# A graph attention layer with gathered rows: E and Q one batch further ahead in two PSUM banks each, the other banks merged

## The chip, the core and the metric

The kernel runs on one NeuronCore of one Trainium2 chip. The metric is the device time of one execution in microseconds, the median of the runs; lower is better. Engines are named as in the profile: PE is TensorE (PEld its weight loads), DVE is VectorE, ACT is ScalarE, POOL is GpSimd, SP is SyncE. PSUM, where PE writes and DVE and ACT read, is used here in eight banks of 128 partitions by 512 float32.

## What is computed

A graph with 6250 nodes of 128 features and 206250 directed edges, sorted by their target node `dst`. Cut to what matters:

```python
Qh = (h @ WQ).reshape(N, 8, 16)          # N = 6250, h = x
Kh = (h @ WK).reshape(N, 8, 16)
Vh = (h @ WV).reshape(N, 8, 16)
Eh = (edge_attr @ WE).reshape(-1, 8, 16) # one row for each edge
score = einsum('ehd,ehd,ehd->eh', Kh[src], Qh[dst], Eh) / sqrt(16)
score = exp(clip(score, -5, 5))
wV = segment_sum(Vh[src] * score[:, :, None], dst)
Z  = segment_sum(score, dst)
x  = layernorm(x + (wV / (Z[:, :, None] + 1e-6)).reshape(N, 128))
```

## The kernel before

**Tiles and batches.** Edges are cut into 1612 tiles of 128, four tiles to a batch (512 edges), 406 batches in all (the last ones are smaller). A table of K and V rows is built in device memory at the start (line 226), and the rows of each edge's source node are fetched from it by `gather` (line 307): four indirect DMAs to a batch, one for each tile, issued by POOL. The first 12 batches (`XB`) fetch rows of x instead and compute K and V themselves in `project` (line 323).

**The loop.** Lines 464 to 516 run over iterations b, and one iteration works on several batches at different stages. Its order on the engines is the order of the calls, written out by hand from b = 12 on (line 466):

- `gather(b)` on POOL (line 475).
- `turn(b-1)` on PE (line 368): four transposes of the product `eq` into a PSUM tile `pps`.
- `stage_a(b)` on PE and ACT (line 348): Q's rows expanded to edges, one matmul into `qps` (line 354), which ACT copies to `qT` in SBUF (line 356); then E, two instructions into `eps` (line 358).
- `finish(q)` in about one of eight iterations (line 404): PE sums the windows of 128 finished nodes into `finps`, ACT copies it to `fin`, and a layernorm of small DVE instructions starts from there (its first writes `rz`, line 604). The layernorm's instructions are dealt out one by one by `fill()`, between the others on DVE, from the next iteration on.
- `stage_b(b-2)` on DVE (line 376): `kq`, the product of gathered K rows and `pps` (line 379), its sum over heads `sc` (382) and the clip (385).
- `messages(b-3)` on DVE (line 411): `msg`, V rows times weights.
- `stage_0(b+AHEAD)` on DVE (line 337): two one-hot matrices, `onehot` (340) for the scatter, `onehotT` (344) for Q.
- `pairs(b)` on DVE (line 361): `eq`, the product of `qT` and `eps` (line 365).
- `weigh(b-2)` on ACT (line 388): two exponentials.
- `stage_c(b-3)` on PE (line 418): the scatter, matmuls of `onehot` and `msg` into `agg` (line 431). A finished sum is copied by ACT (441).
- `q_rows` in about one of eight iterations, always the last thing in its iteration (line 255): Q of 128 more nodes on PE (258), split into three bf16 parts by two ACT casts (261, 263) and two DVE subtractions (262, 264) in turn, and a store to device memory issued by SP (265).

Each engine works through its own instructions in this order; engines wait for each other through semaphores. SP issues all loads ahead of use: `ea` (edge features, six buffers of eight tiles), `relb` (two buffers of sixteen tiles), `qw` (five).

**PSUM banks (lines 207 to 212).** `psE` one bank (`eps`), `psQ` one (`qps`), `psP` two (`pps`), `psT` one, shared under the tag `oT` by `finps`, `qrows`, `project`'s `xtps` and one small count; `psA` two for `agg`, `psX` one for constants.

**The tie (line 317).** From b = 16 on (`LOCK`) the first gather of batch b waits for `expanded[b - lag(b)]`, the Q matmul of line 354 of an earlier batch. `lag` (line 303) falls from 12 at b = 16 by one every four batches down to `STEP` = 1, which it reaches at b = 60. The gathers rotate over `GB` = 17 buffers.

Of the kernel before, what the change touches and what calls it, by code (L numbers as in the profile page):

```python
# [8 lines left out]
F32 = mybir.dt.float32  # L9
# [6 lines left out]
P = 128  # L16
N, E, D, H, DH = 6250, 206250, 128, 8, 16
# [7 lines left out]
MW = D + H  # L25
B = 4
CH = 8
GB = 17
XB = 12
LOCK = XB + 4  # L30
STEP = 1
TAIL = 8
HEAD = 132
NG = (NT + G - 1) // G
AHEAD = 2
EB = 6
SLAG = 2
WT = 8
# [42 lines left out]
def edge_attention(ctx: ExitStack, tc: tile.TileContext, x, xT, srcT, dstT, dstB, dst0, bnd, lo, eaT,  # L81
# [30 lines left out]
    with ExitStack() as fast:  # L112
# [78 lines left out]
        def count_inside():  # L191

            W = 4 * 2 * D
            for a in range(0, NT, W):
                e = min(NT, a + W)
                cl = wp.tile([P, W], F32, name="cl", tag="kvst", bufs=2)[:, :e - a]
                count(P, cl, rel[:, a:e], P - 1)
            nc.vector.tensor_reduce(cn[:, :1], cn, axis=AX.X, op=ALU.add)
            pc = psT.tile([1, 1], F32, name="pc", tag="oT")
            nc.tensor.matmul(pc, cn[:, :1], ones, start=True, stop=True)  # L200
            nc.vector.tensor_copy(cnt_i, pc)

        gp = fast.enter_context(tc.tile_pool(name="gather", bufs=GB))
        ep = fast.enter_context(tc.tile_pool(name="edges", bufs=EB))
        wp = fast.enter_context(tc.tile_pool(name="work", bufs=3))
        sp = fast.enter_context(tc.tile_pool(name="sums", bufs=7))
        psE = fast.enter_context(tc.tile_pool(name="psE", bufs=1, space=bass.MemoryType.PSUM))
        psQ = fast.enter_context(tc.tile_pool(name="psQ", bufs=1, space=bass.MemoryType.PSUM))
        psP = fast.enter_context(tc.tile_pool(name="psP", bufs=2, space=bass.MemoryType.PSUM))
        psT = fast.enter_context(tc.tile_pool(name="psT", bufs=1, space=bass.MemoryType.PSUM))  # L210
        psA = fast.enter_context(tc.tile_pool(name="psA", bufs=2, space=bass.MemoryType.PSUM))
        psX = fast.enter_context(tc.tile_pool(name="psX", bufs=1, space=bass.MemoryType.PSUM))

# [3 lines left out]

        def pair_bank(i, name, shape):

            pool, tag = ((psE, "eps"), (psP, "pps"), (psQ, "qps"), (psP, "pps"))[i % 4]  # L220
            return pool.tile(shape, F32, name=name, tag=tag)


# [24 lines left out]
        nbat = len(batches)  # L248
# [5 lines left out]

        def q_rows(q):
            n = min(P, N - q * P)
            ps = psT.tile([P, D], F32, name="qrows", tag="oT")
            nc.tensor.matmul(ps[:n], xT_sb[:, LEFT + q * P:LEFT + q * P + n], wq_sb, start=True, stop=True)
            st = wp.tile([P, QP, D], BF16, name="qst", bufs=1)
            r1 = wp.tile([P, D], F32, name="qr1", bufs=1)  # L260
            nc.scalar.copy(st[:n, 0, :], ps[:n])  # L261
            nc.vector.tensor_tensor(r1[:n], ps[:n], st[:n, 0, :], op=ALU.subtract)  # L262
            nc.scalar.copy(st[:n, 1, :], r1[:n])
            nc.vector.tensor_tensor(st[:n, 2, :], r1[:n], st[:n, 1, :], op=ALU.subtract)
            nc.sync.dma_start(qs[q * P * QP:(q * P + n) * QP].rearrange("(p s) f -> p s f", s=QP), st[:n])
            built.append(q)
# [20 lines left out]
        chunks, aggs, sums, st8, expanded = {}, {}, {}, {}, {}  # L287
# [15 lines left out]
        def lag(b):  # L303

            return max(STEP, 12 - (b - LOCK) // 4)

# [15 lines left out]

        def project(g, n):

            pt = psT.tile([P, B, P], F32, name="xtps", tag="oT")
            for i in range(n):
                nc.tensor.transpose(pt[:, i, :], g[:, i, :D], ident)
            xgT = wp.tile([P, B, P], F32, name="xgT", tag="kq", bufs=2)
            nc.scalar.copy(xgT[:, :n], pt[:, :n])
            for i in range(0, n, 2):  # L330
                k = min(2, n - i)
                pk = pair_bank(i // 2, "kvps", [P, 2, 2 * D])
                for j in range(k):
                    nc.tensor.matmul(pk[:, j, :], xgT[:, i + j, :], wkv_sb, start=True, stop=True)
                nc.scalar.copy(g[:, i:i + k, :], pk[:, :k, :])

        def stage_0(b):
            t0, n = batches[b][0], len(batches[b])
            oh = wp.tile([P, B, P], F32, name="onehot", bufs=AHEAD + 5)
            nc.vector.tensor_tensor(oh[:, :n], iota_p[:, None, :].to_broadcast([P, n, P]),  # L340
                                    rel[:, t0:t0 + n, None].to_broadcast([P, n, P]), op=ALU.is_equal)
            ohT = wp.tile([QROWS, B * P], BF16, name="onehotT", bufs=AHEAD + 2)
            e0 = t0 % RC * P
            nc.vector.tensor_scalar(ohT[:, :n * P], rels[t0 // RC][:, e0:e0 + n * P], node[:QROWS], None,  # L344
                                    op0=ALU.is_equal)
            st8[b] = oh, ohT

        def stage_a(b, g):
            t0, n = batches[b][0], len(batches[b])
            if b < XB:  # L350
                project(g, n)
            oh, ohT = st8.pop(b)
            pq = psQ.tile([P, B * P], F32, name="qps")
            expanded[b] = nc.tensor.matmul(pq[:, :n * P], loaded[t0 // WT], ohT[:, :n * P], start=True, stop=True)  # L354
            qT = wp.tile([P, B * P], F32, name="qT", bufs=2)
            nc.scalar.copy(qT[:, :n * P], pq[:, :n * P])  # L356
            pe = psE.tile([P, B * P], F32, name="eps")
            nc.tensor.matmul(pe[:, :n * P], we_sb, ea_tiles(t0, n), start=True, stop=True)  # L358
            st8[b] = [n, g, oh, pe, qT]
# [42 lines left out]
                                 start=i == 0, stop=stop and i == len(parts) - 1)  # L402

        def finish(q):
            ps = psT.tile([P, MW], F32, name="finps", tag="oT")
            add_windows(ps, q, True)
            fin = sp.tile([P, MW], F32, name="fin", bufs=2)
            nc.scalar.copy(fin, ps)
            pending.append(layernorm(nc, sp, fin, xbs.pop(q), out, q, stores))
# [36 lines left out]
        gathered = {b: gather(b) for b in range(min(XB, len(batches)))}  # L446
# [11 lines left out]
        def fill():  # L458

            if norms and next(norms[0], None) is None:  # L460
                norms.pop(0)

        held = []
        for b in range(nbat + 4):
            if b >= XB and not manual:
                manual.append(fast.enter_context(tc.manual_schedule()))
            held += [(b + SLAG, store) for store in stores]
            stores.clear()
            if held and (held[0][0] <= b or b >= nbat):
                held.pop(0)[1]()  # L470
            if b < nbat:
                load_chunk(batches[b][0] // CH + EB - 3)
                load_rel(batches[b][0] // RC + 1)
                load_q(batches[b][0] // WT + QLOOK)
                g = gathered.pop(b) if b in gathered else gather(b)
                if b == min(XB, nbat - 1):
                    late_loads()
                if b == min(XB + 8, nbat - 1):
                    relative(C0, NT)
                if b == 14:  # L480
                    from_window(1)
                if b == 0:
                    for i in range(AHEAD):
                        stage_0(i)
                if b > 0:
                    turn(b - 1)
                stage_a(b, g)
            elif b == nbat:
                turn(b - 1)
            norms.extend(pending)  # L490
            pending.clear()
            for q in ready:
                finish(q)
            ready.clear()
            if 0 <= b - 2 < nbat:
                stage_b(b - 2)
            if 0 <= b - 3 < nbat:
                messages(b - 3)
            fill()
            if b + AHEAD < nbat:  # L500
                stage_0(b + AHEAD)
            if b < nbat:
                pairs(b)
            if 0 <= b - 2 < nbat:
                weigh(b - 2)
            if 0 <= b - 3 < nbat:
                stage_c(b - 3)
            fill()
            if b < nbat:
                while len(built) < q_built(min(NJ - 1, batches[b][0] // WT + QLOOK + 2)):  # L510
                    q_rows(len(built))
            if b == min(60, nbat):
                count_inside()
            if b == min(80, nbat + 1):
                inside = nc.values_load(cnt_i[0:1, 0:1], min_val=0, max_val=2 * EPAD,
                                        skip_runtime_bounds_check_because="two counts of EPAD edges")
# [151 lines left out]
```

## Time and profile before

| | |
|---|---|
| runs | 2429.15, 2424.27, 2415.33 us; median 2424.27 us |
| the profiled execution | 2430.0 us, span 2428.1 us, mean granted TensorE clock 0.811 |
| first Q matmul of the loop | 91.3 us after the span's start |
| one batch from b = 60 on, from one `qT` copy to the next | 5.84 us on average |
| one batch from b = 20 to 60 | 5.1 us |
| idle time of DVE before `eq` / `qr` / `rz` | 476.2 / 116.8 / 110.7 us in the whole span |
| mean duration of one `kq`, `sc`, `msg`, `onehot`, `eq` on DVE | 0.68 us each |
| `onehotT` / clip on DVE | 0.36 / 0.20 us |
| one batch on PE at full clock: 4 `pps`, 1 `qps`, 2 `eps`, 8 `agg` | issued over 0.43, 0.22, 0.86 and 0.93 us |

The page's first part is each engine's busy time as a share of the span. No engine is near 100%, so the order of the waits matters, not the sums. Section 5 of the page has the costliest groups of instructions with the idle time before them and what ended it. "remote" there is an event that the profile can't put to an instruction. Matmul ends are modelled by the profiler and not observed.

### The profile page before, as it was taken

What the parts mean: (1) busy time and instruction counts of PE and PEld (TensorE: products, weight loads), DVE (VectorE), ACT (ScalarE), POOL (GpSimd) and SP (SyncE); (2) the same over time, 40 slices, a digit from 0 to 9 for tenths busy, and PEclk for the clock granted to TensorE, in tenths of its full rate; (3) what the DMA queues carried; (4) which work ended last, traced back from release to release, by engine and by line L of the source; (5) the groups of instructions that cost most, each with busy time, mean ns of one, the idle gap of its engine ahead of it and who ended that gap; (6) DMA issues with size and microseconds to landing.
All of it is one profiled execution on the core that took longest, in us unless ns stands there. A gap on an engine that the chain in (4) does not pass through costs nothing.

```text
span 2428.1 us, 24930 instructions
## 1 busy us (share of the span) xinstructions
PE 1539.8 (63%) x6880; PEld 1086.0 (45%) x6880; DVE 1577.4 (65%) x3779; ACT 458.9 (19%) x1572; POOL 1534.0 (63%) x1619
## 2 busy tenths in 40 slices
PE   3587666666665666657666666666666656656665
PEld 2365444444444444444444444444444444444444
DVE  1368778666766666667667666666666667666766
ACT  0232122111111111111111111111111111111111
POOL 7346565666666666666666666666666666666664
PEclk6898898887878888778877878788778788887887
DMA  5645555556554555556456554655555556554642
GB/s 176 201 144 174 179 156 178 165 150 185 170 166 148 168 177 156 164 152 196 147 157 196 160 156 149 184 168 151 169 162 178 147 155 196 157 156 146 197 150 71
DMA packets 178482, 398.16 MB, mean 164 GB/s; under 512 B 61756, under 2 KB 87526, under 8 KB 178336
## 3 DMA queue, kind: packets, MB, share of 16 engines
q0 software_dynamic: 76592, 208.18, 29.4%
q1 hardware_dynamic: 100604, 187.38, 25.2%
q8 instruction: 57, 0.93, 0.2%
q10 hardware_dynamic: 1140, 0.93, 0.1%
q14 instruction: 89, 0.73, 0.1%
HBM read 381.54 MB, written 14.81 MB: 163 GB/s over the span
## 4 chain that ended last, share of the span: by engine, by line
PE 34%; another core or an unknown queue 23%; DVE 19%; issue 16%; ACT 4%; DMA 2%; POOL 1%; DVEq 1%; SPq 0%; ACTq 0%; POOLq 0%
PE agg L431 10%; PE eps L358 10%; PE pps L373 7%; DVE sc L382 4%; DVE kq L379 4%; DVE eq L365 3%; PE qps L354 3%; ACT qT L356 2%; DVE msg L413 2%; PE finps L401 2%; POOL kvrows L314 1%; DVE onehot L340 1%; DVE onehotT L344 1%; DMA kvrows<-kv,src 1%
## 5 line engine op out<-in xcount | busy, mean ns | idle before, releaser
L314 POOL DMA_INDIRECT kvrows<-kv,src x1564 | 1487.1, 951 | 862.3 <-issue 385.6
L431 PEld LDWEIGHTS agg<-msg,onehot 128*128 128x128 f32 x3224 | 516.7, 230 | 664.3 <-issue 520.9
L431 PE MATMUL agg<-msg,onehot 128*128 128x136 f32 x3224 | 560.5, 326 | 352.8 <-DVE msg L413 137.2
L373 PE MATMUL pps<-shift,eq 128*128 128x128 f32 x1612 | 320.5, 332 | 419.6 <-DVE eq L365 238.5
L365 DVE TENSOR_TENSOR eq<-qT,eps 128x512 f32<-128x512 f32 x406 | 276.4, 681 | 476.2 <-ACT qT L356 210.9
L358 PE MATMUL eps<-ea,we_sb 128*128 128x512 f32 (+1 forms) x812 | 528.2, 738 | 16.8 <-issue 13.4
L373 PEld LDWEIGHTS pps<-shift,eq 128*128 128x128 f32 x1612 | 221.4, 168 | 477.4 <-DVE eq L365 282.4
L356 ACT COPY qT<-qps 128x512 f32<-128x512 f32 x406 | 236.8, 583 | 1048.5 <-remote 428.8
L379 DVE TENSOR_TENSOR kq<-kvrows,pps 128x512 f32<-128x512 f32 x406 | 274.8, 677 | 12.1 <-remote 3.5
L413 DVE TENSOR_TENSOR msg<-kvrows,bank 128x512 f32<-128x512 f32 x406 | 274.6, 676 | 9.8 <-ACT bank L391 4.3
L382 DVE TENSOR_REDUCE sc<-kq 128x32 f32<-128x512 f32 x406 | 276.0, 680 | 7.3
L340 DVE TENSOR_TENSOR onehot<-bank,dst_sb 128x512 f32<-128x512 f32 x406 | 275.8, 680 | 0.0
L358 PEld LDWEIGHTS eps<-ea,we_sb 128*128 128x128 f32 x812 | 192.1, 238 | 50.0 <-issue 14.6
L354 PE MATMUL qps<-onehotT,qw 126*128 126x512 bf16 x406 | 187.3, 461 | 0.9 <-ACT qT L356 0.9
L344 DVE TENSOR_SCALAR onehotT<-relb,node 126x512 bf16<-126x512 bf16 x406 | 147.0, 363 | 16.7 <-remote 11.2
L391 ACT ACTIVATE bank<-sc 128x32 f32<-128x32 f32 x406 | 83.0, 204 | 257.2 <-DVE onehot L340 139.8
L401 PEld LDWEIGHTS finps<-sum,shift 128*128 128x128 f32 x478 | 73.1, 215 | 62.4 <-issue 33.9
L401 PE MATMUL finps<-sum,shift 128*128 128x136 f32 x478 | 75.8, 307 | 30.9 <-ACT sum L441 26.2
L262 DVE TENSOR_TENSOR qr<-qrows,qst 128x128 f32<-128x128 f32 (+1 forms) x49 | 14.2, 289 | 116.8 <-ACT qst L261 104.4
L393 ACT ACTIVATE msg<-sc 128x32 f32<-128x32 f32 x406 | 88.0, 217 | 0.0
L385 DVE TENSOR_SCALAR sc<-sc 128x32 f32<-128x32 f32 x406 | 79.2, 195 | 7.3
L441 ACT COPY sum<-agg 128x136 f32<-128x136 f32 x146 | 39.3, 269 | 236.2 <-remote 100.7
(66 smaller groups left out, 525.9 us busy)
## 6 DMA issues: line engine op xcount, KB each, us to landing
ea<-eaT SPq DMA_DIRECT2D x201, 512.0 KB
relb<-relD SPq DMA_DIRECT2D x100, 504.0 KB
kvrows<-kv,src POOLq DMA_INDIRECT x1564
qw<-qs SPq DMA_DIRECT2D x202, 31.5 KB
kv<-kvst SPq DMA_DIRECT2D x12, 512.0 KB
qs<-qst SPq DMA_DIRECT2D x48, 96.0 KB
xb<-x SPq DMA_DIRECT2D x48, 64.0 KB
out<-h SPq DMA_DIRECT2D x48, 64.0 KB
```

The source lines that it names most:

```text
L314: ins = nc.gpsimd.indirect_dma_start(out=g[:k, i, :f], out_offset=None, in_=rows, in_offset=bass.IndirectOffsetOnAxis(ap=src_col(t)[:k], a ...
L340: nc.vector.tensor_tensor(oh[:, :n], iota_p[:, None, :].to_broadcast([P, n, P]), rel[:, t0:t0 + n, None].to_broadcast([P, n, P]), op=ALU.i ...
L354: expanded[b] = nc.tensor.matmul(pq[:, :n * P], loaded[t0 // WT], ohT[:, :n * P], start=True, stop=True)
L356: nc.scalar.copy(qT[:, :n * P], pq[:, :n * P])
L358: nc.tensor.matmul(pe[:, :n * P], we_sb, ea_tiles(t0, n), start=True, stop=True)
L365: nc.vector.tensor_tensor(eq[:, :n * P], qT[:, :n * P], pe[:, :n * P], op=ALU.mult)
L373: nc.tensor.transpose(pp[:, i, :], eq[:, i * P:i * P + P], ident)
L379: nc.vector.tensor_tensor(t1[:, :n], g[:, :n, :D], pp[:, :n], op=ALU.mult)
L382: nc.vector.tensor_reduce(sc[:, :n], t1[:, :n].rearrange("p b (h d) -> p b h d", h=H), axis=AX.X, op=ALU.add)
L401: nc.tensor.matmul(ps, shift[:, P - s:2 * P - s], sums[k], start=i == 0, stop=stop and i == len(parts) - 1)
L413: nc.vector.tensor_tensor(m[:, :n, :D].rearrange("p b (h d) -> p b h d", h=H), g[:, :n, D:].rearrange("p b (h d) -> p b h d", h=H), exp_p[ ...
L431: nc.tensor.matmul(aggs[k], oh[:, i, :], m[:, i, :], start=first and not final, stop=last)
```

## The change

- `stage_a` runs one batch further ahead: iteration b issues `stage_a(b+1)` after `turn(b-1)` (iteration 0 issues both `stage_a(0)` and `stage_a(1)`). `pairs(b)` stays in iteration b, and so uses `qT` and `eps` of the iteration before. `gather(b)` moves behind `stage_a(b+1)` in the order of the calls.
- `psE` and `psQ` have two banks each. `psP` has one, and `psT` is gone: `finps`, `qrows`, `xtps` and the count take their turns in `psE`'s two banks (tag `eps`). `pair_bank` alternates between `psE` and `psQ`.
- `AHEAD` is 3, so `stage_0` also runs one batch further ahead; `onehot` still has seven buffers (`AHEAD + 4`), `onehotT` five, `qT` three.
- `STEP` is 0: from b = 64 on the gather of batch b waits for the Q matmul of batch b itself, which now is issued in iteration b - 1. `GB` is 16.

```diff
-GB = 17
+GB = 16
 XB = 12
 LOCK = XB + 4
-STEP = 1
+STEP = 0
...
-AHEAD = 2
+AHEAD = 3
...
-            pc = psT.tile([1, 1], F32, name="pc", tag="oT")
+            pc = psE.tile([1, 1], F32, name="pc", tag="eps")
...
-        psE = fast.enter_context(tc.tile_pool(name="psE", bufs=1, space=bass.MemoryType.PSUM))
-        psQ = fast.enter_context(tc.tile_pool(name="psQ", bufs=1, space=bass.MemoryType.PSUM))
-        psP = fast.enter_context(tc.tile_pool(name="psP", bufs=2, space=bass.MemoryType.PSUM))
-        psT = fast.enter_context(tc.tile_pool(name="psT", bufs=1, space=bass.MemoryType.PSUM))
+        psE = fast.enter_context(tc.tile_pool(name="psE", bufs=2, space=bass.MemoryType.PSUM))
+        psQ = fast.enter_context(tc.tile_pool(name="psQ", bufs=2, space=bass.MemoryType.PSUM))
+        psP = fast.enter_context(tc.tile_pool(name="psP", bufs=1, space=bass.MemoryType.PSUM))
...
-            pool, tag = ((psE, "eps"), (psP, "pps"), (psQ, "qps"), (psP, "pps"))[i % 4]
+            pool, tag = ((psE, "eps"), (psQ, "qps"))[i % 2]
...
-            ps = psT.tile([P, D], F32, name="qrows", tag="oT")
+            ps = psE.tile([P, D], F32, name="qrows", tag="eps")
...
-            pt = psT.tile([P, B, P], F32, name="xtps", tag="oT")
+            pt = psE.tile([P, B, P], F32, name="xtps", tag="eps")
...
-            oh = wp.tile([P, B, P], F32, name="onehot", bufs=AHEAD + 5)
+            oh = wp.tile([P, B, P], F32, name="onehot", bufs=AHEAD + 4)
...
-            qT = wp.tile([P, B * P], F32, name="qT", bufs=2)
+            qT = wp.tile([P, B * P], F32, name="qT", bufs=3)
...
-            ps = psT.tile([P, MW], F32, name="finps", tag="oT")
+            ps = psE.tile([P, MW], F32, name="finps", tag="eps")
...
-                g = gathered.pop(b) if b in gathered else gather(b)
...
                 if b > 0:
                     turn(b - 1)
-                stage_a(b, g)
+                else:
+                    stage_a(0, gathered[0])
+                if b + 1 < nbat:
+                    stage_a(b + 1, gathered.get(b + 1))
+                st8[b][1] = gathered.pop(b) if b in gathered else gather(b)
```

## The prediction

> **What bounds the kernel now.** The page's sums come first: no engine is near its limit, so a wait sets the pace.
>
> ```profile
> PE 1539.8 (63%) x6880; PEld 1086.0 (45%) x6880; DVE 1577.4 (65%) x3779; ACT 458.9 (19%) x1572; POOL 1534.0 (63%) x1619
> ```
>
> Next, the groups that touch the change, with the idle time before them and what ended it.
>
> ```profile
> L314 POOL DMA_INDIRECT kvrows<-kv,src x1564 | 1487.1, 951 | 862.3 <-issue 385.6
> L365 DVE TENSOR_TENSOR eq<-qT,eps 128x512 f32<-128x512 f32 x406 | 276.4, 681 | 476.2 <-ACT qT L356 210.9
> L356 ACT COPY qT<-qps 128x512 f32<-128x512 f32 x406 | 236.8, 583 | 1048.5 <-remote 428.8
> L379 DVE TENSOR_TENSOR kq<-kvrows,pps 128x512 f32<-128x512 f32 x406 | 274.8, 677 | 12.1 <-remote 3.5
> ```
>
> DVE waits before `eq`, for `qT`, and hardly ever before `kq`, for `pps`. The obvious reading is that 476 us of waiting go when `qT` comes a batch early. What ACT itself waits for says otherwise. This is one stretch of PE, then of ACT, then of POOL, in order of time.
>
> ```profile
> 1255.94 0.38 PE L354 MATMUL qps<-onehotT,qw 126*128 126x512 bf16 x1
> 1256.16 1.02 PE L358 MATMUL eps<-ea,we_sb 128*128 128x512 f32 x2
> 1262.99 1.25 PE L431 MATMUL agg<-msg,onehot 128*128 128x136 f32 x4 [5.81 <-DVE msg L413]
> ```
>
> ```profile
> 1252.76 0.59 ACT L356 COPY qT<-qps 128x512 f32<-128x512 f32 x1 [1.27 <-PE qps L354]
> 1260.97 0.27 ACT L408 COPY fin<-finps 128x136 f32<-128x136 f32 x1 [7.63 <-remote]
> ...
> 1262.53 0.59 ACT L356 COPY qT<-qps 128x512 f32<-128x512 f32 x1 [1.03 <-remote]
> ```
>
> ```profile
> 1245.45 0.95 POOL L314 DMA_INDIRECT kvrows<-kv,src  x1 [2.67 <-remote]
> 1246.70 0.95 POOL L314 DMA_INDIRECT kvrows<-kv,src  x1 [0.31 <-issue]
> ...
> 1259.22 0.95 POOL L314 DMA_INDIRECT kvrows<-kv,src  x1 [0.30 <-issue]
> 1262.76 0.95 POOL L314 DMA_INDIRECT kvrows<-kv,src  x1 [2.60 <-remote]
> ```
>
> The Q matmul is over at 1256.32, ACT sees it at 1262.53, and in between POOL runs out of gathers and pauses. So I cut POOL's list from b = 62 on into runs, wherever it idled over 0.5 us: 78 runs of 12 gathers (three batches), 35 of eight, 29 of four, nine odd ones, none longer. The idle time after them is 2.56, 1.65 and 1.80 us on average. Then I sorted the Q matmuls by how long after a run's start they end, and took the time to ACT's copy. Of 123 in the first 5 us, ten are seen over 0.5 us late. Of 80 from 6 to 8 us nearly all are late, by 2.7 us on average. All 73 from 9 to 15 us are late, and nearly all are seen 2.1 to 3.1 us after the last gather of the run. The start shows the same at full length: POOL issues 16 gathers untied from 96 to 116 us, and ACT waits 12.07 us for PE, until 117.42.
>
> That gives the pace. A gather is issued every 0.95 + 0.30 = 1.25 us, so a batch costs 5.01 us plus its share of a pause: three batches 14.74 + 2.56 = 17.30 us (5.77 each), two 11.38 (5.69), one 6.51. Weighted with their counts this is 5.81, against 5.84 measured. POOL pauses because the tie lets a batch go only once its Q matmul is *seen*, and Q matmuls late in a run are seen after the run. **What counts is how many ties are seen between a pause and about 5 us (late ones about 9 us) into the next run, not how long DVE waits.**
>
> The Trainium skill ("Perfetto Trace Analysis", the section on the Tensor Engine instruction) says that a matmul's end in the profile is computed, and that its semaphore goes out when PSUM has acknowledged the write. The 6 us above fit neither part, as the next PE work had started long before; by that rule alone the whole 476 us would go.
>
> **The change part by part.** Take a release at time 0. PE, ACT and DVE hold still, and the last `pps`, `qps`, `eps` become visible.
>
> *E and Q ahead (bought by two banks each).* Before: ACT copies `qT` (0.59), DVE does `eq` (0.69), PE four transposes and the Q matmul (0.82 us at full clock, 1.54 at half, from the PE rows), so the second tie is seen at 2.3 to 2.9 us. After: `eq` was done during the pause. But `kq` waits for the same release, since `pps` ran just before `qps` and is seen with it. And with **one `psP` bank** the next transposes wait for that `kq`. So 0.65 + 0.82 or 1.54 = 1.5 to 2.3 us: 0.6 to 0.8 earlier. The third follows one DVE iteration later. That iteration is 5 x 0.6 (pitch of the large instructions) + 0.7 + 0.3 = 4.0 us, so the third comes at about 5.5 to 6.3 instead of 6 to 7. The fourth, near 9.5, is in the zone where everything is seen after the run. So three batches stay the most. The gain is fewer single runs: 15 of the 29 have no `q_rows` near their start; all of these turned into triples would save 15 x (6.51 - 5.77) = 11 us; none, nothing. I take 11.
>
> *The first 60 batches.* Here POOL is held by the falling lag, and DVE idles 28 us before `eq` from 200 to 414 us. Half of it goes: **-15**, bounds 0 and -28.
>
> *`q_rows` in `psE`.* `qr` and `qst` stand on DVE ahead of the next `kq`. Before, `turn` needed only `eq`, so the next Q matmul was done during a pause and its tie was there at the release. Now `turn` waits for `kq`, behind `qr`. Where `qrows` itself is caught in a pause, the release is followed by two ACT casts and two DVE subtractions (1.3 us in the rows), `kq` (0.65), transposes and Q (0.82 to 1.54): POOL restarts some 3 us later. Before, such an event gave a single run instead; 14 single runs have a `qr` in their first 5 us. So 14 x (3.0 - 0.74) = **+32**. Bounds: 0 if `qrows` is always seen in time, 41 x 3 = +123 if never.
>
> *`finps` in `psE`.* Both banks hold an `eps` when it is issued, so it waits for `eq`, 2 to 3 us later than now, with `agg` queued behind it on PE, and then `turn`; `rz` on DVE and the exponentials on ACT stand behind `fin`. Where this falls late in a run, `rz` sits out the pause and the next tie comes too late: a third of 41 events, 14 x 0.74 = **+10**, bounds 0 and 41 x 0.74 = 30. `eps` of the next batch, which waits for `fin`'s copy, has an iteration's cover; without that it would cost the wait before `eq` again.
>
> *`AHEAD` 3 with seven `onehot` buffers.* Seven are now in use at once, so DVE's `onehot` waits for the scatter of one iteration ago, before of two. That is a PE completion, so it can be caught in a pause. Then `onehot`, `onehotT` and `eq` (1.6 us) come after the release and the second tie at 3.1 to 3.9. Of ties from 3 to 4 us 28% are late, which makes a single run. If half of some 113 pauses (340 batches in threes) go so: 56 x 0.28 = 16, x 0.74 = **+12**, bounds 0 and 24.
>
> *At nothing:* `GB` 16 and `STEP` 0 (gather b is tied to the Q matmul of the same iteration as before, and its rows lie ready 7 us before `kq`); `relb` wanted an iteration earlier (issued 13 us or more ahead, landed in 4.9 at the median); the start's bank changes, by which four banks still take turns.
>
> Sum: 2430.0 - 15 - 11 + 32 + 10 + 12 = 2458 in the profile's terms, whose execution lies 0.24% above the median; so **2452 us**, 1.1% slower. By the bounds of its terms 2385 to 2600.
>
> The skill has one more voice against the change ("TensorE: Matmul & The Clock Gate", HAM oscillation): adding PSUM double-buffering gave a kernel no further gain. No run here shows it yet; it would leave 2424.
>
> **Rivals.**
> *More ties for each run (faster).* If the earlier third tie lets a fourth through, runs of four batches cost 15 x 1.25 + 0.95 + 2.56 over 4 = 5.57 us: 333 x (5.57 - 5.81) = -80, with the start's 15 **about 2330**. Without pauses the floor is 5.01, 2140 us. For it: the loop kept 5.1 us from b = 20 to 60, where gathers were spread. Against: not one run longer than 12 while the tie held. It decides if the fourth Q matmul ends within 5 us of a run's start; mild forms (more pairs at 5.69) give 2385 to 2410.
> *Single runs become the rule (much slower).* The bank `psP` and the rotation of `psE` put `kq`, `qr`, `fin` and `onehot` ahead of a tie. If the second tie comes later than the 4.7 us that a single run lasts, in half of the batches: 333 x 0.5 x 0.70 = +117, **2540**; always, 2657. Against: its price above is 3.9 at worst in an ordinary iteration.
> *The pace stays (no change).* Pairs and triples cost nearly the same, so a moved tie within them changes nothing: **2424**. For it: exactly that flatness.
>
> **How the numbers follow.** Forecast (2436 to 2490) 0.33, single runs (above 2490) 0.18, pace stays 0.19, more ties 0.30. A difference under 0.5% is about what cannot be told from no change: faster 0.30, same 0.19, slower 0.51. The range 2340 to 2550 leaves out runs of four as the rule and singles beyond half; the forecast's own is 2436 to 2490.
>
> **What would show it.** The idle time before `eq` should fall below 150 us, that before `kq` rise above 100, with more before `onehot`, `qr` and `rz`. No run of POOL should exceed 12 gathers, and pauses of 5 us should appear at `q_rows`. Runs of 16 gathers or more would make the prediction wrong to the fast side; single runs above 60, or long PE waits of the transposes for `kq`, to the slow side.

## The result, and the profile after

The changed kernel takes 2463.23 us (median of 4, 2459.33 to 2472.52), the kernel before 2422.96 us on the same chip: a ratio of 1.0168, 95% interval 1.0145 to 1.0190. It is 1.7% slower; 2452 us, or 1.1%, were forecast. Its profiled span is 2462.3 us against 2428.1, 34.2 us more.

The first part of the page after, and its groups (duration sums, mean ns, then the idle time before the group and what ended most of it):

```profile
PE 1526.7 (62%) x6880; PEld 1095.0 (44%) x6880; DVE 1572.0 (64%) x3779; ACT 463.6 (19%) x1572; POOL 1529.8 (62%) x1619
...
L313 POOL DMA_INDIRECT kvrows<-kv,src x1564 | 1483.2, 948 | 899.5 <-issue 388.5
L372 PE MATMUL pps<-shift,eq 128*128 128x128 f32 x1612 | 314.9, 328 | 690.9 <-DVE kq L378 404.3
...
L339 DVE TENSOR_TENSOR onehot<-bank,dst_sb 128x512 f32<-128x512 f32 x406 | 276.2, 681 | 276.5 <-remote 182.2
L378 DVE TENSOR_TENSOR kq<-kvrows,pps 128x512 f32<-128x512 f32 x406 | 275.0, 677 | 137.9 <-remote 50.8
L364 DVE TENSOR_TENSOR eq<-qT,eps 128x512 f32<-128x512 f32 x406 | 274.1, 675 | 6.0 <-ACT qT L355 2.5
```

The change does what it says: DVE's 476 us of waiting before `eq` are down to 6. They did not become time. 126 us of them stand before `kq` now, 277 before `onehot`, 66 before `qr` (182.6 against 116.8) and 32 before `rz` (142.4 against 110.7). The transposes wait 271 us longer, and what ends most of it is `kq`. Nearly the same busy time lies in a longer span, and POOL idles 37 us more.

Where the time goes is seen in POOL's instructions by stretch of time. First the kernel before, then the changed one (window in us, its length, busy time and number of instructions, granted clock, DMA share, GB/s):

```profile
0.00:420.00 420.00, 237.65 (x255) 0.84 0.57 173
420.00:1000.00 580.00, 376.83 (x397) 0.81 0.56 166
1000.00:1600.00 600.00, 391.24 (x412) 0.80 0.55 164
1600.00:2400.00 800.00, 520.76 (x548) 0.81 0.55 162
```

```profile
0.00:420.00 420.00, 229.84 (x248) 0.80 0.55 166
420.00:1000.00 580.00, 373.68 (x394) 0.81 0.56 165
1000.00:1600.00 600.00, 380.13 (x402) 0.80 0.55 162
1600.00:2400.00 800.00, 517.51 (x547) 0.81 0.56 164
```

Seven instructions are missing at 420 us, three more by 1000, ten more from 1000 to 1600. So there are two losses: one at the start, and one that comes in bursts. The second is found by listing POOL's pauses over 3.1 us after b = 62. Before there is one, 4.61 us long. After there are fifteen, and in fourteen of them DVE's `qr` stands 3.4 us ahead of POOL's next gather. What they have beyond an ordinary pause of 2.56 us sums to 33.6 us, against 2.0. This is one of them, in order of time, all engines:

```profile
1236.37 0.68 DVE L364 TENSOR_TENSOR eq<-qT,eps 128x512 f32<-128x512 f32 x1
...
1237.11 0.49 PE L257 MATMUL qrows<-wq_sb,xT_sb 128*128 128x128 f32 x2 [0.26 <-issue]
...
1243.22 0.95 POOL L313 DMA_INDIRECT kvrows<-kv,src  x1 [0.30 <-issue]
1246.46 0.27 ACT L260 CAST qst<-qrows 128x128 bf16<-128x128 f32 x1 [4.02 <-remote]
1246.75 0.29 DVE L261 TENSOR_TENSOR qr<-qrows,qst 128x128 f32<-128x128 f32 x1 [9.64 <-ACT qst L260]
...
1247.41 0.29 DVE L263 TENSOR_TENSOR qst<-qr,qst 128x128 bf16<-128x128 f32 x1 [0.36 <-ACT qst L262]
1247.62 0.69 DVE L378 TENSOR_TENSOR kq<-kvrows,pps 128x512 f32<-128x512 f32 x1
...
1248.36 1.12 PE L372 MATMUL pps<-shift,eq 128*128 128x128 f32 x4 [10.76 <-DVE vh L618]
...
1249.27 0.63 PE L353 MATMUL qps<-onehotT,qw 126*128 126x512 bf16 x1
...
1249.94 0.58 ACT L355 COPY qT<-qps 128x512 f32<-128x512 f32 x1 [2.56 <-PE qps L353]
1250.18 0.94 POOL L313 DMA_INDIRECT kvrows<-kv,src  x1 [6.01 <-PE qps L353]
```

The Q rows' matmul is over at 1237.60 and is seen 8.9 us later, 2.3 us after the run's last gather. Two casts and two subtractions follow, then `kq`, which had stood behind them on DVE; only then may the transposes use the one `psP` bank, and the next Q matmul stands behind them on PE. POOL is let go 3.7 us after the release. The transposes' releaser is named `vh`, but `kq`, which ended at 1248.31, is what frees their bank.

In the kernel before, Q's rows are caught in a pause as often, and the pause stays an ordinary one. One such case:

```profile
1171.71 0.38 PE L258 MATMUL qrows<-wq_sb,xT_sb 128*128 128x128 f32 x2
...
1174.84 0.63 PE L354 MATMUL qps<-onehotT,qw 126*128 126x512 bf16 x1
...
1180.17 0.27 ACT L261 CAST qst<-qrows 128x128 bf16<-128x128 f32 x1 [8.36 <-remote]
...
1180.50 0.95 POOL L314 DMA_INDIRECT kvrows<-kv,src  x1 [2.55 <-remote]
...
1181.34 0.68 DVE L379 TENSOR_TENSOR kq<-kvrows,pps 128x512 f32<-128x512 f32 x1
```

The next Q matmul was over before the pause, so its end comes into sight at the release as well, and POOL starts 0.3 us after the cast and ahead of `kq`. This happens 13 times after b = 62 in this trace, each in a pause of 2.3 to 2.6 us. In the changed kernel it is ten times, and POOL starts 3.7 us after the cast in each.

### The profile page after: what moved, and what is told of

It is laid out like the page before. It is cut to its first block, busy times and chain, and to the rows that moved or that the text cites. A ratio compares the mean times of both kernels' runs of the same rounds, so it can differ in the third digit from the quotient of the medians.

```text
span 2462.3 us, 24547 instructions
## 1 busy us (share of the span) xinstructions
PE 1526.7 (62%) x6880; PEld 1095.0 (44%) x6880; DVE 1572.0 (64%) x3779; ACT 463.6 (19%) x1572; POOL 1529.8 (62%) x1619
## 4 chain that ended last, share of the span: by engine, by line
PE 29%; DVE 29%; another core or an unknown queue 16%; issue 15%; DMA 4%; POOL 3%; ACT 2%; DVEq 1%; ACTq 0%; POOLq 0%; SPq 0%
PE agg L430 9%; PE eps L357 8%; DVE kq L378 6%; PE pps L372 5%; DVE eq L364 5%; DVE sc L381 5%; DVE msg L412 4%; POOL kvrows L313 3%; DVE onehotT L343 3%; PE finps L400 3%; DMA kvrows<-kv,src 3%; DVE onehot L339 3%; PE qps L353 3%; PE kvps L333 1%
## 5 line engine op out<-in xcount | busy, mean ns | idle before, releaser
L372 PE MATMUL pps<-shift,eq 128*128 128x128 f32 x1612 | 314.9, 328 | 690.9 <-DVE kq L378 404.3
L430 PE MATMUL agg<-msg,onehot 128*128 128x136 f32 x3224 | 542.7, 320 | 8.8 <-DVE msg L412 4.1
L400 PE MATMUL finps<-sum,shift 128*128 128x136 f32 x478 | 90.9, 353 | 72.2 <-DVE eq L364 67.6
L400 PEld LDWEIGHTS finps<-sum,shift 128*128 128x128 f32 x478 | 80.3, 249 | 119.6 <-DVE eq L364 108.2
L261 DVE TENSOR_TENSOR qr<-qrows,qst 128x128 f32<-128x128 f32 (+1 forms) x49 | 14.3, 291 | 182.6 <-ACT qst L260 130.8
L606 DVE TENSOR_SCALAR rz<-fin 128x8 f32<-128x8 f32 x48 | 9.8, 203 | 141.7 <-ACT fin L407 80.0
```

The source lines that it names most:

```text
L372: nc.tensor.transpose(pp[:, i, :], eq[:, i * P:i * P + P], ident)
L400: nc.tensor.matmul(ps, shift[:, P - s:2 * P - s], sums[k], start=i == 0, stop=stop and i == len(parts) - 1)
L430: nc.tensor.matmul(aggs[k], oh[:, i, :], m[:, i, :], start=first and not final, stop=last)
```

## The experiments

The chip was found in two conditions, and this has to be known to read them: in the one the kernel before took 2423 to 2452 us, in the other 2043, always the same for kernels that ran together; the chip numbered 1 on record was found in both. I call them **late** and **prompt**, by what the traces show below. The forecast and its result are of the late condition. Ratios are always to the kernel before, run beside the kernel on the same chip. The changed kernel itself ran in the late condition only; in the prompt one there are variants of it.

**Eight onehot buffers** (prompt condition, as the next three).

```
-GB = 16
+GB = 15
-            oh = wp.tile([P, B, P], F32, name="onehot", bufs=AHEAD + 4)
+            oh = wp.tile([P, B, P], F32, name="onehot", bufs=AHEAD + 5)
```

> The changed kernel with eight onehot buffers in place of seven (paid by one gather buffer less), so that onehot waits for the scatter of two iterations ago, as before. My theory, a tie seen too late for its run of gathers: the term of +12 us (bounds 0 and +24) goes, so about 2451 us, 2439 to 2463, and DVE's idle time before onehot, 276 us, falls below 50 us and turns up before kq and eq instead. Rival, DVE's idle time is the loss: most of the 276 us come back and the kernel is faster than the one before, below 2410 us.

2074.36 us against 2043.42, ratio 1.0155 (1.0138 to 1.0172). DVE's wait before `onehot` is 0.0 us here, but with seven buffers it is 0.0 to 1.1 us in the next three variants as well: in the prompt condition there is no such wait to take away. The rival's large gain did not come; the price of this wait in the late condition stays open.

**Q rows ahead of the loop in psP.**

```
-            ps = psE.tile([P, D], F32, name="qrows", tag="eps")
+            pool, tag = (psE, "eps") if manual else (psP, "pps")
+            ps = pool.tile([P, D], F32, name="qrows", tag=tag)
```

> The changed kernel with the Q rows that are made ahead of the loop put in the bank psP, which the K and V table no longer uses, in place of psE, where they stand behind the table. The first copy of qT came at 91.7 us before and at 121.5 us after. My theory of the start: this wait is why the first 60 batches cost +12 us where I had -15; first copy of qT back to 92 to 97 us, b = 60 at 399 to 414 us instead of 426, and the total 2463 - (12 to 27) = 2436 to 2451 us. Rival, the start is hidden: POOL's gathers and the falling lag set the times up to b = 80 anyway (both kernels reach it at 535 us), and the total stays within 5 us of 2463.

2061.46 us, ratio 1.0092 (1.0076 to 1.0109): 13 us less than the variant above, whose Q rows start behind the table as in the changed kernel. ACT's first copy of `qT` comes at 52 us instead of 75, b = 60 at 319 instead of 332, and that distance stays to the end.

**Two psP banks, one psQ bank.**

```
-        psQ = fast.enter_context(tc.tile_pool(name="psQ", bufs=2, space=bass.MemoryType.PSUM))
-        psP = fast.enter_context(tc.tile_pool(name="psP", bufs=1, space=bass.MemoryType.PSUM))
+        psQ = fast.enter_context(tc.tile_pool(name="psQ", bufs=1, space=bass.MemoryType.PSUM))
+        psP = fast.enter_context(tc.tile_pool(name="psP", bufs=2, space=bass.MemoryType.PSUM))
...
-            pool, tag = ((psE, "eps"), (psQ, "qps"))[i % 2]
+            pool, tag = ((psE, "eps"), (psP, "pps"))[i % 2]
```

> The changed kernel with two psP banks and one psQ bank (the table takes its turns in psE and psP). The transposes of a batch no longer wait for the kq of the batch before; Q's bank is free as soon as ACT has copied qT. My theory: what is lost at q_rows is the chain qr, qst, kq, transposes, Q matmul ahead of the next tie. With kq out of it the thirteen pauses of 3.2 to 6.0 us go (their excess over an ordinary pause sums to 33 us), and PE's idle time before the transposes, 691 us, falls to near the 420 us of before: 2463 - 33 = 2430 us. If also the third and fourth tie come before the run's zone of late ends, runs of 16 gathers appear and it is below 2410 us. Rival, the onehot buffers and the shared E bank hold the pace: 2455 to 2465 us.

2072.89 us, ratio 1.0149 (1.0132 to 1.0165). PE's wait before the transposes falls to 63.9 us, from 541.5 in the variant above, and nothing is gained by it: from b = 100 on both take 5.0 us a batch. The prompt condition has no pauses of 6 us to take away, so their cause is not tested here.

**A bank for Q's rows and the sums alone, one psQ bank.**

```
-        psQ = fast.enter_context(tc.tile_pool(name="psQ", bufs=2, space=bass.MemoryType.PSUM))
+        psQ = fast.enter_context(tc.tile_pool(name="psQ", bufs=1, space=bass.MemoryType.PSUM))
...
+        psT = fast.enter_context(tc.tile_pool(name="psT", bufs=1, space=bass.MemoryType.PSUM))
...
-            pool, tag = ((psE, "eps"), (psQ, "qps"))[i % 2]
+            pool, tag = ((psE, "eps"), (psQ, "qps"), (psE, "eps"), (psP, "pps"))[i % 4]
...
-            ps = psE.tile([P, D], F32, name="qrows", tag="eps")
+            ps = psT.tile([P, D], F32, name="qrows", tag="oT")
...
-            ps = psE.tile([P, MW], F32, name="finps", tag="eps")
+            ps = psT.tile([P, MW], F32, name="finps", tag="oT")
```

> The changed kernel with one psQ bank, and the bank that this frees given to Q's rows and the sums (qrows, finps) alone, as they had one before. E stays ahead in two banks, Q ahead too (its bank is free as soon as qT is copied). My theory: the terms of +32 us (q_rows behind kq) shrinks, since qrows need not wait for eq, but qr still stands on DVE ahead of kq, so a part of it stays; the term of +10 us (finps) goes, and the start's 12 to 27 us come back: 2463 - 10 - 12 - (0 to 32) = 2409 to 2441 us. DVE's idle time before rz, 142 us, falls to about 110 us, and PE's before finps, 72 us, to about 31 us. Rival, one psP bank and seven onehot buffers hold the pace: 2450 to 2463 us.

2044.09 us, ratio 1.0001 (0.9992 to 1.0011): in the prompt condition the loss that the other variants have is undone. PE's wait before `finps` is 0. The gain lies ahead of b = 80: b = 60 comes at 305 us, against 319 with the Q rows ahead of the loop in psP and 332 without; afterwards all three run at the same pace.

**The changed kernel, and the kernel before, in the late condition.** No edit.

> The changed kernel as it is, beside the four variants, for which the kernel before took 2043 us and not 2423. In their traces no Q matmul is seen late (0.04 us to ACT's copy of qT, against 2.2), POOL issues 1354 gathers without a pause, and a batch takes the 5.01 us that I called the floor. Theory: where nothing is seen late, POOL's own issuing sets the pace from b = 80 on, and the change costs only what it loses by then: like the variant with eight onehot buffers, ratio 1.012 to 1.018, about 2074 us, first copy of qT at 75 us and b = 100 at 520 to 530 us. Where Q matmuls are seen late again, 2463 us and ratio 1.017. Rival, one psP bank or seven onehot buffers cost something in every batch: over 5.05 us per batch from b = 100 to 380 although nothing is seen late.

> The kernel before, for a trace beside the others. Theory: at 2043 us POOL issues 1612 gathers at 1.25 us from first to last, with less than 10 us of pauses in all, the first copy of qT comes near 52 us and b = 100 near 501 us, as in the variant with a bank for Q's rows and the sums. Rival, it gets there in another way, with pauses and an earlier start. Where Q matmuls are seen late again, 2423 us and the runs of 12, 8 and 4 gathers as in the first trace.

2490.81 against 2452.36 us, ratio 1.0178 (1.0149 to 1.0207), and 2450.71 us for the profiled run of the kernel before. So the result repeats. The changed kernel has eight pauses over 3.1 us here (21.7 us beyond the ordinary ones), seven of them 3.4 us after a `qr`; the kernel before has one (2.1 us).

**Half of the gathers as plain loads** (the kernel before, late condition).

```
             for i, t in enumerate(batches[b]):
                 k = min(P, (E - t * P + 63) // 64 * 64)
...
+                if b >= LOCK and i >= 2:
+                    nc.sync.dma_start(g[:k, i, :], kv[t % 48 * P:t % 48 * P + k, :])
+                    continue
```

> The kernel before, with two of the four gathers of a batch (from b = 16 on) replaced by plain loads of the same size from rows in order, on SP's queue. It leaves out the gathering of half of the rows: their K and V are those of other nodes. POOL then issues two gathers in 2.5 us for each batch, and the bytes moved stay. Theory: gathers set the pace, by their issuing at 1.25 us or by hiding the ends of matmuls: the pace from b = 100 to 380 falls from 5.0 (or 5.8) to between 3.9 and 4.6 us per batch, where DVE's 3.9 us of work for a batch or PE's bound it, and the total to 1650 to 1900 us; with two gathers in a run no Q matmul ends more than 3 us after its start, so none is seen late. Rival, the DMA engines or the chain of a batch set the pace: it stays above 4.9 us.

1711.28 us (one run) against 2452.36. Of 338 Q matmuls not one is seen more than 0.04 us after its end (the kernel before, run beside it: 197 more than 0.5 us, 2.15 us on average over all 338). The condition was late here too: up to b = 16 nothing is replaced, and the first `qT` comes at 96.4 us, as in the late traces of the kernel before (91.7 and 94.1); in the prompt condition it came at 52 and 75 us. POOL from 1200.75 us on (start, duration, in brackets the idle time before and what ended it), and DVE's and DMA's share in the loop (window, then busy time of PE, PEld, DVE, ACT, POOL, clock, DMA share, GB/s):

```profile
1200.75 0.94 POOL L317 DMA_INDIRECT kvrows<-kv,src  x1 [1.60 <-PE qps L357]
1202.00 0.95 POOL L317 DMA_INDIRECT kvrows<-kv,src  x1 [0.30 <-issue]
1204.59 0.94 POOL L317 DMA_INDIRECT kvrows<-kv,src  x1 [1.64 <-DMA kvrows<-kv]
```

```profile
829.00:1600.00 771.00, 600.04 (x3260) 406.25 (x3258) 748.40 (x1820) 217.96 (x739) 374.16 (x397) 0.99 0.83 248
```

With two gathers in a run, a batch costs 3.89 us and DVE is busy 97% of the time, so DVE is the next bound. The DMA engines are busier than before (83% against 55%), so it is not their whole load that hides the ends of matmuls. That leaves POOL's unbroken gathers; but their number is halved too, and this run does not part the length of a run from the rate of gathers.

**A memset between gathers** (the kernel before, late condition).

```
+    spacer = cp.tile([P, 8], F32, name="spacer")
...
+                if b >= LOCK:
+                    nc.gpsimd.memset(spacer, 0.0)
```

> The kernel before, with one small memset (128x8) on POOL after each gather from b = 16 on (one gather buffer less pays for nothing but is kept at 17). Theory: where Q matmuls are seen late, it is the unbroken row of gathers that hides them; with a memset between two gathers they are seen within 1 us, POOL no longer pauses at the tie, and a batch costs 4 x (1.25 + the memset's own time of 0.1 to 0.3 us) = 5.4 to 6.2 us. Where nothing is seen late, POOL sets the pace and every memset adds its whole time: 1550 x 0.1 to 0.3 = 155 to 465 us more than 2043. Rival, lateness has nothing to do with what POOL runs: as late as before, and a batch costs its 5.84 us plus four memsets.

2460.30 (one run) against 2452.36 us. POOL's timeline:

```profile
1201.86 0.95 POOL L315 DMA_INDIRECT kvrows<-kv,src  x1 [0.19 <-issue]
1202.82 0.12 POOL L323 MEMSET spacer<- 128x8 f32 x1
1203.12 0.95 POOL L315 DMA_INDIRECT kvrows<-kv,src  x1 [0.19 <-issue]
```

The memset fits into the 0.30 us between two gathers: the pitch stays 1.26 us. The Q matmuls are as late as before (190 of 338 over 0.5 us, 2.25 us on average over all). My theory is wrong in this: another instruction between gathers does not help when the pitch stays. Longer gaps were not tried.

**Own bank, and two psP banks, again.** The prompt condition once more.

> The variant with one psQ bank and a bank for Q's rows and the sums alone once more. Where the kernel before takes some 2440 us and Q matmuls are seen late (the changed kernel: ratio 1.017 and 1.018). Theory: the Q rows no longer wait for eq to free a bank, so their matmul is over before POOL's run hides it; of the pauses over 3.1 us, 14 and 7 of them in the two traces of the changed kernel and worth 34 and 22 us, most go, and so does the late start (first qT near 93 us, worth 8 to 12 us at b = 60): ratio 1.000 to 1.008. Rival, the chain qr, kq, transposes, Q matmul makes the pauses, whatever bank Q's rows have: they stay, only the start comes back, ratio 1.011 to 1.015. Where the kernel before takes 2043 us: ratio 1.000 again, by the start alone.

> The variant with two psP banks and one psQ bank once more. Where the kernel before takes some 2440 us: the transposes, and so the Q matmul behind them, no longer wait for the kq of the batch before, while Q's rows keep the bank of E. Theory, the pauses over 3.1 us come from the chain through kq: they go, the late start stays: ratio 1.003 to 1.010. Rival, they come from the bank that Q's rows share with E: they stay, ratio 1.014 to 1.020. If the earlier Q matmuls also let more than three batches through in a run, runs of 16 gathers appear and the ratio is below 1. Where the kernel before takes 2043 us: ratio 1.015 again, by the start alone.

Own bank 2044.32 against 2043.94 us, 1.0000 (0.9990 to 1.0010); two psP banks 2071.20 us, 1.0132 (1.0115 to 1.0149). As before, and no word on the pauses.

**Own bank, in the late condition.**

> The variant with one psQ bank and a bank for Q's rows and the sums alone a third time, because it has only run where the kernel before takes 2043 us and no Q matmul is seen late. If the kernel before takes some 2440 us: theory, most of the pauses over 3.1 us (34 and 22 us in the two traces of the changed kernel) go and the start comes back, ratio 1.000 to 1.008; rival, the chain through kq makes them whatever the bank, 1.011 to 1.015. If the kernel before takes 2043 us: ratio 1.000.

2450.03 against 2423.09 us, ratio 1.0134 (1.0089 to 1.0179): the rival's figure. The start comes back (first `qT` 92.2 us, b = 60 at 405.2, the kernel before 414.5 in its first trace), but the pauses stay: ten over 3.1 us, nine of 5.83 to 5.95 us that all follow a `qr` by 3.4 us, 30.7 us in all. One of them, in order of time:

```profile
1131.22 0.39 PE L258 MATMUL qrows<-wq_sb,xT_sb 128*128 128x128 f32 x2
...
1138.21 0.27 ACT L261 CAST qst<-qrows 128x128 bf16<-128x128 f32 x1 [6.95 <-remote]
...
1139.37 0.69 DVE L379 TENSOR_TENSOR kq<-kvrows,pps 128x512 f32<-128x512 f32 x1
...
1141.02 0.63 PE L354 MATMUL qps<-onehotT,qw 126*128 126x512 bf16 x1
...
1141.93 0.95 POOL L314 DMA_INDIRECT kvrows<-kv,src  x1 [5.92 <-DVE y L622]
```

It is the same chain, though the bank now belongs to Q's rows alone. So the shared E bank is not what makes these pauses. Nor are the casts at the head of the release by themselves, which stand there in the kernel before as well, with POOL 0.3 us behind them; a Q matmul that was still to come is what differs.

**Two psP banks, with the Q rows ahead of the loop in psP.** The edits of the second and the third variant together.

> The changed kernel with two psP banks, one psQ bank, and the Q rows made ahead of the loop in psP: the only variant in which a batch's transposes and Q matmul do not wait for the kq of the batch before. If the kernel before takes some 2440 us and Q matmuls are seen late: theory, the pauses of 5 to 6 us come from the chain qr, qst, kq, transposes, Q matmul; here the Q matmul is over before the release, so none over 4 us that follows a qr by 3.4 us is left (9 to 14 of over 3.1 us in the three traces with one psP bank), POOL's idle time after b = 62 falls from 308 to 325 us to 280 to 300 us, the start comes back as in the variant with a bank for Q's rows (b = 60 at 405 to 414 us), and the ratio is 0.995 to 1.005. Rival, the casts that ACT and DVE do at the head of the release make the pauses, whatever bank kq holds: they stay, and the ratio is 1.010 to 1.016. If the kernel before takes 2043 us: 1.006 to 1.010, the drag of E's shared bank on the first 60 batches alone.

2071.35 against 2043.99 us, ratio 1.0130 (1.0113 to 1.0147), the prompt condition again. The forecast of 1.006 to 1.010 missed by an oversight of mine: in this variant the K and V table takes its turns in psP, so the Q rows stand behind it there as they did in psE (first `qT` at 74.5 us, 52 in the second variant). So no run takes `kq` out of the chain while matmuls are seen late.

## Why the prediction was right, and in which terms it was not

**The mechanism held.** POOL's gathers and the late sight of matmuls set the pace, and DVE's 476 us before `eq` were not time to be gained. No run of POOL is longer than 12 gathers, as forecast, and single runs fell from 29 to 20 while pairs rose from 35 to 49 (43 to 38 and 60 to 65 in the second pair of traces). The experiment with half of the gathers shows that gathers set the pace: with two in a run, no late matmul and 3.89 us a batch.

The terms, taken from ACT's copies of `qT` (first, b = 60, last) and the ends of the traces, in us against the trace of the kernel before (the second column against the one that ran beside it):

| step | forecast | result | changed kernel, second time | own bank, late condition |
|---|---|---|---|---|
| up to b = 60 | -15 | +11.2 | +8.1 | -9.3 |
| pauses at `q_rows` beyond 2.56 us | +32 | +31.6 | +19.7 | +28.7 |
| rest of the loop (single runs, `finps`, `onehot`) | +11 | -11.4 | -3.4 | -13.6 |
| after the last `qT` | 0 | +2.8 | +2.9 | +2.8 |
| sum | +28 | +34.2 | +27.3 | +8.5 |

(Each is a difference of two single profiled executions, and so good to a few us at best. The first: 425.7 - 414.5; the second 33.6 - 2.0; the loop in all (2445.2 - 425.7) - (2413.9 - 414.5) = +20.1, less 31.6; the tail 17.1 - 14.3; rounded last. The last column is the fastest of its four runs, 2438.4 us, against the first trace of the kernel before; by the medians that variant lost 27 us, so this column shows only a part of its loss.)

The changed kernel copies `qT` one batch further ahead, so these copies are not quite the same mark in both. By POOL's gathers, the result's column is +9.9 up to the first gather of b = 64, +23.3 from there to the end of the last one and +1.0 after it: the split stands, and most of the last row's 3 us is that shift. Both kernels copy `qT` of b = 80 at 534 us, but that does not mean that the start is made good: the first gather of that batch is issued at 527.4 before and at 537.2 after.

**q_rows behind kq: right in mechanism and in the price of one event; the number was in part luck.** POOL starts 3.7 us after the cast, against 0.3 in the kernel before: 3.4 us later, where some 3 were forecast. The forecast was 14 pauses and there were fourteen, but only nine are longer than 5 us (29 of the 33 us); in the second trace there were seven, five of them long. And the +32 has the single runs that such events gave before already taken off (14 x 0.74 = 10), the +31.6 has not: single runs with a `qr` fell from 14 to 4, worth 7 us at that price. Like for like the row is some +24, and the row below it -4. One reason of the step was off: "where `qrows` itself is caught in a pause" suffices, and its bank plays no part, as the own bank showed. That the next Q matmul has to wait through the release is shown by the comparison with the kernel before; that `kq` is what holds it is read from the chain in the traces and was not shown by taking it out.

**The start: the step that failed.** It was costed "at nothing: ... the start's bank changes, by which four banks still take turns". True of the table, but not of the Q rows built ahead of the loop, which moved into one of these four banks. These are the first Q rows' matmuls, changed kernel and own bank, both in the late condition:

```profile
88.13 0.38 PE L257 MATMUL qrows<-wq_sb,xT_sb 128*128 128x128 f32 x2
```

```profile
17.01 0.38 PE L258 MATMUL qrows<-wq_sb,xT_sb 128*128 128x128 f32 x2
```

They now stand behind the whole table, and the first `qT` comes 30 us later (121.5 against 91.7 in the kernel before). With the own bank the first 60 batches gain 9 us, inside the bounds of 0 to -28 that this step had; so a gain of that kind was there, 9 of the 15 us, and the missed term is some +20 us (425.7 against 405.2 at b = 60, though the two kernels differ in more than this bank). In the prompt condition moving the Q rows alone gave 13 us, to the end.

**The rest was too dear.** -11, +10 and +12 were to sum to +11; -3 to -14 came out. The waits themselves are there (`onehot` 277 us, `finps` 72 against 31, `rz` +32), but the single runs that they were to cost are not: the three terms made 15 fewer, 14 more and 16 more of the 15 without a `qr`, so 30, and some 17 came. The runs do not part the three. The right total thus rests in part on luck: a missed loss at the start (+26 beside the forecast) and too high a price in the loop (-22 by the table) nearly cancel.

**The rivals.** More ties for each run: no run over 12 gathers in the result's trace (in the prompt condition up to 1355, but there nothing is late). Single runs as the rule: no, 20 of them where over 60 were to show it. Its other sign, long waits of the transposes for `kq`, did come (404 us) without its price; in the prompt condition, too, 541 us of waiting before the transposes went with 5.0 us a batch. The pace stays: no, 1.0168 and 1.0178 both exclude it. The page "TensorE: Matmul & The Clock Gate" of the Trainium skill (HAM oscillation), by which PSUM double-buffering gave a kernel no further gain, is borne out only in part: no gain anywhere, 1.000 with the own bank in the prompt condition, but a loss in the late one.

No variant beats the kernel before. The own bank equals the kernel before in the prompt condition and is 1.3% slower in the late one.

## What to carry to other kernels

Before a waiting engine is freed, ask what lets the slowest issuer go: here moving DVE's wait only lengthened the chain ahead of POOL's tie. When a tile moves into a shared bank, follow it through every phase, the start included; a producer that had a bank of its own may now queue behind a whole table. And look in every trace for the condition of the chip: with all of the change but eight `onehot` buffers the prompt condition showed a loss at the start alone, while in the late one the steady loop lost more than the start.

## What the hardware showed that was not expected

**The same program took 16% less time in one condition of the chip** (2043 against 2423 to 2452 us). The own bank's traces of both kinds part the two. Every gather takes the same 0.95 us and the DMA queues move the same bytes. What differs is the sight of TensorE's ends, and the granted clock (0.80 and 0.86 from 425 us on). The clock alone does not explain it: in the late trace 144 of 221 Q matmuls that took the short 0.38 to 0.45 us are seen over 0.5 us late, in the prompt one none of the 82 that took longer. First the prompt, then the late condition: Q matmuls and the copies that wait for them, amid gathers.

```profile
1202.91 0.38 PE L354 MATMUL qps<-onehotT,qw 126*128 126x512 bf16 x1
...
1203.33 0.58 ACT L356 COPY qT<-qps 128x512 f32<-128x512 f32 x1 [2.35 <-PE qps L354]
...
1207.77 0.38 PE L354 MATMUL qps<-onehotT,qw 126*128 126x512 bf16 x1
...
1208.19 0.59 ACT L356 COPY qT<-qps 128x512 f32<-128x512 f32 x1 [2.97 <-PE qps L354]
```

```profile
1200.29 0.38 PE L354 MATMUL qps<-onehotT,qw 126*128 126x512 bf16 x1
...
1204.01 0.59 ACT L356 COPY qT<-qps 128x512 f32<-128x512 f32 x1 [5.27 <-PE agg L431]
...
1206.38 0.63 PE L354 MATMUL qps<-onehotT,qw 126*128 126x512 bf16 x1
...
1211.18 0.59 ACT L356 COPY qT<-qps 128x512 f32<-128x512 f32 x1 [6.35 <-PE agg L431]
```

In the prompt condition each copy starts 0.04 us after the matmul, for all 338 from b = 62 on, though POOL issues gathers at 1.25 us, up to 861 in one row. In the late one, 3.34 and 4.17 us. In the prompt condition the loop is bound by POOL's issuing alone: 4 x 1.25 = 5.0 us a batch, the floor of the forecast, measured 5.02. The start shows the difference too: in both, POOL issues its first 48 gathers in one row up to 64 us, and from 20 to 60 us PE, which builds the table, is busy for 12.5 us in the late trace and for 28.5 in the prompt one. The first `qT` comes at 92.2 and at 52.1 us.

**Only TensorE's ends are late, as far as the traces show it.** In the late traces, more than 6 us into a run of gathers, and where that was the last thing waited for, PE's transposes follow DVE's `kq` or `eq` after 0.06 us, the scatter follows `msg` after 0.15, DVE's `qr` follows ACT's `qst` after 0.03 (medians), while `qT` follows the Q matmul after 3.6 to 4.6. What makes the condition late is not known: nothing in the program differs, and it was not in my hands.
